# A recommender's attention over a history of 200: a fifth tile of rows fetched by address, a reordered step, and a contraction of the head over 128 rows

## The chip, the cores and the metric

The kernel runs on one core of a Trainium2 chip. The core has a matrix engine (PE, with its weight loads shown as PEld), a vector engine (DVE), an activation engine (ACT), GpSimd (POOL) and a synchronizing engine (SP). ACT, POOL and SP each have a queue of their own on which DMAs are issued in order. The metric is the device time of one execution in microseconds (us). The kernel before has a median of 31618.79 over three runs (31618.49 to 31619.22).

## What is computed

The reference is a "deep interest" ranking model for a batch of B = 16384 with a history of L = 200 items. Embeddings have 64 numbers. For every position l of the history and every sample, an attention unit of 36 hidden values weighs the row of the item; dice normalizes over axis 1 of the hidden values, that is over the batch, for each l by itself.

```python
u = u_emb[user]; it = i_emb[item]; c = c_emb[cate]
h = i_emb[hist]                                   # (200, 16384, 64)
itb = jnp.broadcast_to(it[None], h.shape)
feat = jnp.concatenate([h, itb, h - itb, h * itb], axis=-1)
a = dice(feat @ au_W1 + au_b1, au_alpha, axis=1)  # 36 hidden values
w = a @ au_W2 + au_b2
cur = jnp.sum(w * jax.lax.stop_gradient(h), axis=0)
z = jnp.concatenate([u, it, c, cur], axis=-1)
z = dice(z @ W1 + b1, alpha1, axis=0)
z = dice(z @ W2 + b2, alpha2, axis=0)
return z @ W3 + b3
```

`dice(x)` is `x * (p + alpha * (1 - p))` with p the sigmoid of x normalized by its mean and variance. So 200 x 16384 rows of 256 bytes are to be fetched from a table of 100000 rows, at random places.

## The kernel before

**Tiling.** The batch is cut into 128 tiles of 128 samples. Sixteen tiles (TD) make a chunk c; there are ND = 8 chunks for each l. One chunk of one l is a step, k = 8 l + c, so there are 1600 steps. Steps are software pipelined: in the code of step k, rows of chunk k are fetched, chunk k - 1 is transposed and multiplied, the result of k - 2 is taken out of PSUM and measured, and chunk k - LAG, whose normalization is known by then, gets its gate and its weights (LAG is 10). The first 180 l run in a hardware loop, `tc.For_i`, of 45 l an iteration; the other 20 follow it, and then the head. The order of the instructions on every engine is the order in which the code issues them (`tc.manual_schedule`).

**Rows.** `gather` (line 125) is one indirect DMA on POOL's queue that fetches the 128 rows of one tile into a slice of `rows[k % 5]`. In four of the eight chunks (SIDES) the last tile is not gathered in this way. Its rows are fetched one at a time by address: `scale_addresses` (L146) multiplies the indices by the bytes of a row, `addresses` (L268) loads some of them into registers of an engine, and each row is a DMA of 256 bytes. SP does so for the chunks 1 and 5 (`rows_by_sync`, L280, 16 registers at a load) into the buffers `side`; it is asked one or two chunks ahead by `ask`, 32 rows a step. ACT does so for the chunks 3 and 7 (`rows_by_scalar`, L291, 8 registers at a load) into `aside`, 16 rows behind the gate and 16 behind hidden of each step. ACT's rows count on a semaphore `landed`, which `await_rows_by_scalar` (L297 to L299) waits for and clears. `turn` copies the finished tile into `rows` (L339, ACT) right ahead of the transposes.

**A step.** In the order of issue: `fetch(k)` on POOL; `gate(k - LAG)`, a sigmoid on ACT (L312) from `xs` to PSUM `pg`; `weights(k - LAG)`, y = pg * xs on DVE (L315) and eight passes of PE into `wb`; half of ACT's rows; `hidden(k - 2)` on ACT (L323), px with the bias into `xs[k % XR]`, and `measure` (L328), two statistics on DVE; the other half of ACT's rows; `turn(k - 1)`, the copy, four 64x512 transposes on DVE (L154) into `hT[k % LAG]`, four PE passes with a unit matrix into `ph` and eight into `px` (L159, `layer`); `weigh(k - LAG)` on DVE (L319, L320), which adds weight times row to `curT`; `product(k - 1)`, hm = ph * itT on DVE (L345) and four passes into `px`. At the last chunk of an l `moments` (L351 to L365 on DVE, then a root on ACT at L168 and L169, L170 on DVE) gives scale and shift for the gate.

**Buffers.** Five `rows`, LAG = 10 `hT`, XR = 9 `xs`, one `px`, `ph`, `pg` and `wb` in PSUM.

**Head.** 256 gathers for users and categories, the first layer (`head_layer`), its moments (L503 to L511), and then for each of eight chunks `dice` (L522 on ACT, L523 and L524 on DVE), the second layer (L538 with `w2a` over 128 rows, L539 with `w2b` over a quarter of 32 rows), L541 on ACT and statistics (L467). The third layer follows (L159 again) and the output.

Of the kernel before, what the change touches and what calls it, by code (L numbers as in the profile page):

```python
# [14 lines left out]
P = 128  # L15
D = 64
EPS = 1e-8
CH = 512
# [1 line left out]
CD = 2 * CH  # L20
LPB = 45
ROWS = 5
LAG = 10
XR = 9
IDX = 3
BY_SP = (1, 5)
BY_ACT = (3, 7)
SIDES = (1, 3, 5, 7)
LOAD = 16
GROUP = 8  # L30
ROW = 4 * D
U8 = mybir.dt.uint8

# [2 lines left out]
def din_kernel(  # L36
# [32 lines left out]
    ZA = P // 2  # L69
    ZB = Z1 - ZA  # L70
    NS = len(SIDES)
    NB, NA = len(BY_SP), len(BY_ACT)
    serial = iter(range(10**6))
    NC = NT - NS
    BODY = L - L % LPB if L > LPB else 0
# [6 lines left out]
    def make(name, *shape, dt=F32):  # L82
        return const.tile(list(shape), dt, name=name)
# [29 lines left out]
    idx = [make(f"idx{i}", P, NC, dt=I32) for i in range(IDX)]  # L113
    ids = [make(f"ids{i}", P, NT, dt=I32) for i in range(3)]
    side = [make(f"side{i}", P, D) for i in range(3)]
    aside = [make(f"aside{i}", P, D) for i in range(3)]
    landed = [tc.alloc_semaphore(f"landed{i}") for i in range(3)]
    addrs = make("addrs", 2 * S + 1, NS * P, dt=I32)
    addr = [addrs[i * S : i * S + 1] for i in range(3)]
# [98 lines left out]
    w1a = make("w1a", P, 4, P)  # L218
    w1b = make("w1b", P, 4, S)
    w2a = make("w2a", P, P)  # L220
    w2b = make("w2b", P, P)
    w3 = make("w3", P, 4, P)
    b1a = make("b1a", P, 1)
    b1b = make("b1b", S, 1)
# [9 lines left out]
    def head_weights():  # L234
        for t in (w1a, w1b, w2a, w2b, w3, bias2, al2):
            nc.vector.memset(t, 0.0)
        w1 = W1.rearrange("(f d) z -> d f z", d=D)
        for e in range(2):
            for g in range(2):
                r, d = quarter(e, g), ts(e, S)  # L240
                nc.sync.dma_start(w1a[r, :, ts(g, ZA)], w1[d, :, :ZA])
                nc.sync.dma_start(w1b[r, :, ts(g, ZB)], w1[d, :, ZA:])
        for g in range(2):
            nc.sync.dma_start(w2a[ts(g, ZA), g * ZA : g * ZA + Z2], W2[:ZA])
            nc.sync.dma_start(b1a[ts(g, ZA)], col(b1)[:ZA])
            nc.sync.dma_start(ala[ts(g, ZA)], col(alpha1)[:ZA])
            nc.sync.dma_start(b1b[ts(g, ZB)], col(b1)[ZA:])
            nc.sync.dma_start(bias2[g * ZA : g * ZA + Z2], col(b2))
            nc.sync.dma_start(al2[g * ZA : g * ZA + Z2], col(alpha2))
            for j in range(4):  # L250
                r = slice(j * S + g * ZB, j * S + (g + 1) * ZB)
                nc.sync.dma_start(w2b[r, g * ZA : g * ZA + Z2], W2[ZA:])
                w = j * S + g * ZO
                nc.sync.dma_start(w3[g * ZA : g * ZA + Z2, j, w : w + ZO], W3)
                nc.sync.dma_start(alb[r], col(alpha1)[ZA:])
        nc.sync.dma_start(bias3, b3.partition_broadcast(P))
        for t, u in ((ala, al1a), (alb, al1b), (al2, al12)):
            nc.vector.tensor_scalar(u, t, -1.0, 1.0, ALU.mult, ALU.add)

        for t, n in ((same_a, ZA), (same_b, ZB)):  # L260
            nc.vector.tensor_single_scalar(lane, lanes, n - 1, ALU.bitwise_and)
            nc.vector.tensor_copy(t, lane)
            nc.vector.tensor_scalar(t, t, 0.0, n / P, ALU.is_equal, ALU.mult)

    flat = i_emb.rearrange("v d -> (v d)").bitcast(U8)

    def addresses(l, s, p0, n, engine):
        _, at = nc.values_load_multi_w_load_instructions(  # L268
            addr[l % 3][:, s * P + p0 : s * P + p0 + n],
            engines=(engine,), min_val=0, max_val=ROW * (V - 1),  # L270
            skip_runtime_bounds_check_because="the DMA checks the address against the table",
        )
        return [flat[ds(a, ROW)].rearrange("(o d) -> o d", o=1) for a in at]

    def rows_by_sync(m, part, n):
        l, j = divmod(m, NB)
        s, dst = SIDES.index(BY_SP[j]), side[m % 3].bitcast(U8)
        for p0 in range(part * n, part * n + n, LOAD):
            for j, row in enumerate(addresses(l, s, p0, LOAD, mybir.EngineType.SP)):
                nc.sync.dma_start(dst[p0 + j : p0 + j + 1], row)  # L280


    keys = {}

    def rows_by_scalar(m, part):
        l, j = divmod(m, NA)
        s, dst = SIDES.index(BY_ACT[j]), aside[m % 3].bitcast(U8)
        key = keys.setdefault(m, f"rows{next(serial)}")
        for j, row in enumerate(addresses(l, s, part * GROUP, GROUP, mybir.EngineType.Activation)):
            p = part * GROUP + j  # L290
            dma = nc.scalar.dma_start(dst[p : p + 1], row).then_inc(landed[m % 3], 16)  # L291
            tc.no_tile_sem_insts.add(dma.ins.name)
            tc.add_to_no_dep_group(key, dma.ins)

    def await_rows_by_scalar(m):
        if m in keys:
            fence = nc.scalar.wait_ge(landed[m % 3], 16 * P)  # L297
            tc.declare_fence(fence.ins, group=keys.pop(m))
            nc.scalar.sem_clear(landed[m % 3])  # L299
# [4 lines left out]
    def fetch(k):  # L304
        l, c = divmod(k, ND)
        for n in range(TD - has_side(k)):
            j = column(c, n)
            gather(rows[k % ROWS], idx[l % IDX][:, j : j + 1], n, i_emb)
# [13 lines left out]
    def hidden(k):  # L322
        nc.scalar.activation(xs[k % XR], px, AF.Identity, bias=au_bias)  # L323
# [3 lines left out]
        for i in range(2):  # L327
            nc.vector.bn_stats(stats[l % 3][:, 2 * c + i, :], xs[k % XR][:, ts(i, CH)])  # L328

    def turn(k):  # L330
        if has_side(k):
            l, c = divmod(k, ND)
            if c in BY_ACT:
                m = l * NA + BY_ACT.index(c)
                await_rows_by_scalar(m)
                of = aside[m % 3]
            else:
                of = side[(l * NB + BY_SP.index(c)) % 3]
            nc.scalar.copy(rows[k % ROWS][:, TD - 1], of)  # L339
        transpose(hT[k % LAG], rows[k % ROWS])  # L340
        layer(ph, [(unit, hT[k % LAG])])
        layer(px, [(blk_h, hT[k % LAG]), (blk_i, itT[k % ND])], last=False)
# [25 lines left out]
    def step(k, last=None):  # L368

        def has(j):  # L370
            return last is None or j <= last

        if has(k):
            fetch(k)
        if has(k - LAG):
            gate(k - LAG)
            weights(k - LAG)
        if has(k):
            scalar_rows(k, 0)
        if has(k - 2):  # L380
            hidden(k - 2)
            measure(k - 2)
        if has(k):
            scalar_rows(k, 1)
        if has(k - 1):
            turn(k - 1)
        if has(k - LAG):
            weigh(k - LAG)
        if has(k - 1):
            product(k - 1)  # L390
        if has(k - 2) and (k - 2) % ND == ND - 1:
            moments((k - 2) // ND)

    AHEAD = ND // NB - 1 - BY_SP[0]

    def ask(k, end):
        m, part = divmod(k + 1 + AHEAD, ND // NB)
        if m < end * NB:  # L400
            rows_by_sync(m, part, P * NB // ND)

    def scalar_rows(k, slot):
        m, part = divmod(k, ND // NA)
        n = P * NA // ND // GROUP
        for i in range(n)[slot::2]:
            rows_by_scalar(m, part * n + i)

    def steps(l0, n, end):
        for k in range(n * ND):  # L410
            l, c = divmod(k, ND)
            if c == 0 and l + 1 < end:
                load_hist_ids((l + 1) % IDX, l0 + l + 1)
            if c == 2 and l + 1 < end:
                load_addresses((l + 1) % 3, l0 + l + 1)
            if c == 4 and l + 1 < end:
                scale_addresses((l + 1) % 3)
            ask(k, end)
            step(k)

    with tc.manual_schedule():
# [4 lines left out]
        load_ids(ids[2], r_user)  # L426
        nc.gpsimd.iota(lanes, pattern=[[1, P]], base=P, channel_multiplier=-1)
        attention_weights()
        for t in (*hT, *xs, *side, *aside, hm):
            nc.vector.memset(t, 0.0)  # L430
        for t in curT:
            nc.vector.memset(t, 0.0)
# [14 lines left out]
            if c:  # L447
                transpose(itT[c - 1], rows[(c - 1) % ROWS])
        nc.vector.memset(rows[-1 % ROWS], 0.0)
        for k in range(-1 - AHEAD, 0):  # L450
            ask(k, L)
        head_weights()

    if BODY:
        with tc.For_i(0, BODY, LPB) as l0:  # L455
            with tc.manual_schedule():
                steps(l0, LPB, LPB + 1)
                await_rows_by_scalar(LPB * NA - 1)

    K = (L - BODY) * ND  # L460
    za = [hT[(K - LAG + c) % LAG] for c in range(ND)]
# [28 lines left out]
    with tc.manual_schedule():  # L490
# [36 lines left out]
        z2 = itT  # L527
        na, nb = head_moments(0, same_a), head_moments(1, same_b)
        ab = ucT[:2]
        for j in range(2):  # L530
            dice(ab[j], zb[j], nb, al1b, alb)
        for c in range(ND + 1):
            if c < ND:
                dice(curT[c], za[c], na, al1a, ala)
                q = ts(c % 4, S)
                for h in range(2):
                    cols = ts(h, CH)
                    nc.tensor.matmul(pz[c % 4][:, cols], w2a, curT[c][:, cols], start=True, stop=False)  # L538
                    nc.tensor.matmul(pz[c % 4][:, cols], w2b[q], ab[c // 4][q, cols], start=False, stop=True)  # L539
            if c:  # L540
                nc.scalar.activation(z2[c - 1], pz[(c - 1) % 4], AF.Identity, bias=bias2)  # L541
                measure_head(2, c - 1, z2[c - 1])

        n2 = head_moments(2, same_a)
        for c in range(ND):
# [56 lines left out]
```

## Time and profile before

| what | us |
|---|---|
| median of three runs | 31618.79 |
| the profiled execution | 31616.96 |
| its span | 31615.1 |
| POOL busy | 23766.1 |
| PE busy | 20448.2 |
| DVE busy | 15015.4 |
| ACT busy | 4479.6 |
| DMA engines, mean busy share: POOL's queue, the two others with rows | 11.8%, 0.4% and 0.3% |

Busy time does not count register loads or the issuing of DMAs: the time that ACT and SP spend on issuing rows is in none of these. An ordinary line of a group reads: line, engine, operation, output <- inputs, count | busy us in all, mean ns of one | idle time of the engine before them, and what ended it. "issue" is idle time that ended without a wait for anything that the profile shows. A line of a timeline reads: start and duration in us, engine (with a q: its queue, issuing), line, operation, tiles, how many were merged into the line, and in brackets the idle time before it and who released it. In a line on one place of the code, three times separated by strokes are the minimum, median and maximum in ns.

### The profile page before, as it was taken

How to read it: one execution, taken by the hardware profiler on the slowest of the kernel's cores; microseconds unless marked ns; L12 is line 12 of the kernel's file. 1: busy time of each engine (PE TensorE's matmuls, PEld its weight loads, DVE VectorE, ACT ScalarE, POOL GpSimd, SP SyncE). 2: the span in 40 equal slices, each digit the busy share in tenths (PEclk: the TensorE clock that was granted, in tenths of full speed). 3: DMA queues.
4: the chain of work that ended last, by engine and by line, in shares of the span. 5: the costliest groups of instructions: out<-in, count | busy, mean ns of one | idle time of the engine just before them, and what ended most of it. 6: DMA issues, size and time to landing. Idle time of an engine off the chain costs nothing. (4 is left out here: it accounts for less than half of the span.)

```text
span 31615.1 us, 357535 instructions
## 1 busy us (share of the span) xinstructions
PE 20448.2 (65%) x38864; PEld 8357.2 (26%) x38864; DVE 15015.4 (47%) x18963; ACT 4479.6 (14%) x4670; POOL 23766.1 (75%) x25189
## 2 busy tenths in 40 slices
PE   5666666666666666666666666666666666666666
PEld 2222222222222222222222222222222222222222
DVE  4444444444444444444444444444444444444443
ACT  1111111111111111111111111111111111111111
POOL 7777777777777777777777777777777777777776
PEclk7888888888888888888888888888888888888887
DMA  1111111111111111111111111111111111111111
GB/s 29 28 28 28 28 28 28 28 28 28 28 28 28 28 28 28 28 28 28 28 28 28 28 28 28 28 28 28 28 28 28 28 28 28 28 28 28 28 28 23
DMA packets 1050292, 890.26 MB, mean 28 GB/s; under 512 B 644640, under 2 KB 644640, under 8 KB 1047784
## 3 DMA queue, kind: packets, MB, share of 16 engines
q0 software_dynamic: 805888, 826.84, 11.8%
q1 hardware_dynamic: 138920, 27.05, 0.4%
q10 hardware_dynamic: 102976, 13.32, 0.3%
q14 instruction: 2202, 18.04, 0.2%
q8 instruction: 306, 5.01, 0.1%
HBM read 865.03 MB, written 0.13 MB: 27 GB/s over the span
## 5 line engine op out<-in xcount | busy, mean ns | idle before, releaser
L125 POOL DMA_INDIRECT rows<-in_L_rec_i_emb,idx x24800 | 23403.2, 944 | 7593.5 <-issue 7032.1
L159 PE MATMUL ph<-hT,unit 128*128 128x512 f32 x6404 | 5658.4, 1029 | 10498.9 <-DVE hT L154 10498.9
L154 DVE STREAM_TRANSPOSE hT<-rows 64x512 f32<-64x512 f32 x6404 | 4518.8, 706 | 8256.8 <-DMA rows<-in_L_rec_i_emb,idx 4150.3
L328 DVE BATCH_NORM_STATS2 st<-xs 128x6 f32<-128x512 f32 x3204 | 2060.4, 685 | 7172.9 <-ACT xs L323 7172.9
L159 PEld LDWEIGHTS ph<-hT,unit 128*128 128x128 f32 x6404 | 1688.5, 295 | 13506.4 <-DVE hT L154 13334.4
L159 PE MATMUL px<-hT,blk_h 128*128 128x512 f32 x6404 | 3936.6, 702 | 0.0
L323 ACT ACTIVATE xs<-px,au_bias 128x1024 f32<-128x1024 f32 x1602 | 1784.3, 1114 | 14626.1 <-PE px L159 12323.9
L159 PE MATMUL wb<-y,blk_p 128*128 128x512 f32 x6440 | 3329.8, 599 | 455.3 <-DVE y L315 455.3
L159 PE MATMUL px<-itT,blk_i 128*128 128x512 f32 x6404 | 3368.8, 608 | 0.0
L159 PE MATMUL wb<-xs,blk_x 128*128 128x512 f32 x6440 | 3307.3, 595 | 51.5 <-PEq L455 39.9
L159 PE MATMUL px<-hm,blk_m 128*128 128x512 f32 x6408 | 3013.0, 592 | 40.5 <-DVE hm L430 40.5
L312 ACT ACTIVATE pg<-xs,sh,rs 128x1024 f32<-128x1024 f32 x1610 | 1939.8, 1205 | 3751.2 <-issue 2579.9
L315 DVE TENSOR_TENSOR y<-pg,xs 128x1024 f32<-128x1024 f32 x1610 | 1956.6, 1215 | 512.9 <-ACT pg L312 508.6
L159 PEld LDWEIGHTS px<-hT,blk_h 128*128 128x128 f32 x6404 | 1566.7, 245 | 2295.1 <-issue 2294.6
L319 DVE SCALAR_TENSOR_TENSOR wb<-wb,au_bias,hT 128x1024 f32<-128x1024 f32 x1610 | 2080.5, 1292 | 88.2 <-PE wb L159 36.0
L320 DVE TENSOR_TENSOR curT<-wb,curT 128x1024 f32<-128x1024 f32 x1610 | 1970.8, 1224 | 54.8
L345 DVE TENSOR_TENSOR hm<-ph,itT 128x1024 f32<-128x1024 f32 x1601 | 1941.2, 1212 | 0.0
L159 PEld LDWEIGHTS px<-itT,blk_i 128*128 128x128 f32 x6404 | 1374.9, 215 | 1925.3 <-issue 1925.3
L159 PEld LDWEIGHTS wb<-y,blk_p 128*128 128x128 f32 x6440 | 1212.0, 191 | 2081.7 <-issue 1445.9
L159 PEld LDWEIGHTS wb<-xs,blk_x 128*128 128x128 f32 x6440 | 1228.3, 191 | 1603.9 <-issue 1597.9
L159 PEld LDWEIGHTS px<-hm,blk_m 128*128 128x128 f32 x6408 | 1218.1, 190 | 1573.0 <-issue 1424.7
L339 ACT COPY rows<-aside 128x64 f32<-128x64 f32 x401 | 97.9, 244 | 2659.6 <-DMA aside<-in_L_rec_i_emb 2525.7
(155 smaller groups left out, 2171.5 us busy)
## 6 DMA issues: line engine op xcount, KB each, us to landing
aside<-in_L_rec_i_emb ACTq DMA_DIRECT2D x51200, 0.2 KB
side<-in_L_rec_i_emb SPq DMA_DIRECT2D x51200, 0.2 KB
rows<-in_L_rec_i_emb,idx POOLq DMA_INDIRECT x24800, 2.4
idx<-in_r_hist SPq DMA_DIRECT2D x200, 62.0 KB
addrs<-in_r_hist SPq DMA_DIRECT2D x200, 2.0 KB
rows<-in_L_rec_i_emb,ids POOLq DMA_INDIRECT x128, 2.4
rows<-in_L_rec_c_emb,ids POOLq DMA_INDIRECT x128, 2.4
rows<-in_L_rec_u_emb,ids POOLq DMA_INDIRECT x128, 2.4
```

What stands on the lines that cost most here:

```text
L125: nc.gpsimd.indirect_dma_start(out=dst[:, n, :], out_offset=None, in_=table, in_offset=bass.IndirectOffsetOnAxis(ap=ids, axis=0),)
L154: nc.vector.transpose(by_tile(dst[ts(e, D)], i), of[ts(i, D), :, ts(e, S)])
L159: nc.tensor.matmul(dst[:, ts(i, CH)], lhsT, rhs[:, ts(i, CH)], start=(first and j == 0), stop=(last and j == len(pairs) - 1), skip_group_c ...
L312: nc.scalar.activation(pg, xs[k % XR], AF.Sigmoid, bias=shifts[i], scale=rstds[i])
L315: nc.vector.tensor_mul(y, pg, xs[k % XR])
L319: nc.vector.scalar_tensor_tensor(wb, wb, au_bias2, hT[k % LAG], ALU.add, ALU.mult)
L320: nc.vector.tensor_add(curT[k % ND], wb, curT[k % ND])
L323: nc.scalar.activation(xs[k % XR], px, AF.Identity, bias=au_bias)
L328: nc.vector.bn_stats(stats[l % 3][:, 2 * c + i, :], xs[k % XR][:, ts(i, CH)])
L339: nc.scalar.copy(rows[k % ROWS][:, TD - 1], of)
L345: nc.vector.tensor_mul(hm, ph, itT[k % ND])
```

## The change

Chunks with a side tile become 1, 3, 4, 6 and 7: five tiles of each l are fetched by address, and 123 are gathered. SP and ACT both fetch rows of every such tile: each step has 80 rows, of which SP issues the first 40 and ACT the last 40, in loads of 20 registers. All count on `landed`, the buffers are three `side`, and `aside` is gone. The rows of a tile are no longer asked for ahead: those of step k are issued in step k, at the end of what ACT has in it. The copy has a function of its own, `place`, ahead of the rows.

In a step `hidden` now comes first; in the step where an l ends, its statistics and moments follow at once. Then come the gate, the copy, the rows, the transposes with their passes, the statistics of other steps, the product, and at the end `weights` and `weigh`. LAG is 9 and XR is 8.

In the head `w2b` has four planes of 128 rows, of which one quarter is not zero, so that the second matmul contracts over 128 rows as the first does; the `dice` of `ab` is made where it is needed, behind the first pass of a group of four chunks, and the result is taken out of PSUM two chunks later instead of one.

```diff
-LAG = 10
-XR = 9
+LAG = 9
+XR = 8
-BY_SP = (1, 5)
-BY_ACT = (3, 7)
-SIDES = (1, 3, 5, 7)
-LOAD = 16
-GROUP = 8
+SIDES = (1, 3, 4, 6, 7)
+LOAD = 20
...
-    w2b = make("w2b", P, P)
+    w2b = make("w2b", P, 4, P)
...
+    PER_STEP = NS * P // ND
+
+    def rows_by_address(k):
+        l, s = divmod(k, ND)
+        for i, (engine, issue) in enumerate(
+            ((mybir.EngineType.SP, nc.sync), (mybir.EngineType.Activation, nc.scalar))
+        ):
+            n = PER_STEP // 2
+            for r0 in range(s * PER_STEP + i * n, s * PER_STEP + (i + 1) * n, LOAD):
+                _, at = nc.values_load_multi_w_load_instructions(
+                    addr[l % 3][:, r0 : r0 + LOAD],
+                    engines=(engine,), min_val=0, max_val=ROW * (V - 1),
...
+                for r, a in enumerate(at, r0):
+                    m, p = l * NS + r // P, r % P
+                    key = keys.setdefault(m, f"rows{next(serial)}")
+                    dma = issue.dma_start(
+                        side[m % 3].bitcast(U8)[p : p + 1],
+                        flat[ds(a, ROW)].rearrange("(o d) -> o d", o=1),
+                    ).then_inc(landed[m % 3], 16)
...
-    def turn(k):
+    def place(k):
         if has_side(k):
             l, c = divmod(k, ND)
...
-            nc.scalar.copy(rows[k % ROWS][:, TD - 1], of)
+            m = l * NS + SIDES.index(c)
+            await_rows(m)
+            nc.scalar.copy(rows[k % ROWS][:, TD - 1], side[m % 3])
+
+    def turn(k):
         transpose(hT[k % LAG], rows[k % ROWS])
...
+        ends = (k - 2) % ND == ND - 1
         if has(k):
             fetch(k)
+        if has(k - 2):
+            hidden(k - 2)
+            if ends:
+                measure(k - 2)
+                moments((k - 2) // ND)
         if has(k - LAG):
             gate(k - LAG)
-            weights(k - LAG)
+        if has(k - 1):
+            place(k - 1)
         if has(k):
-            scalar_rows(k, 0)
-        if has(k - 2):
-            hidden(k - 2)
-            measure(k - 2)
-        if has(k):
-            scalar_rows(k, 1)
+            rows_by_address(k)
         if has(k - 1):
             turn(k - 1)
-        if has(k - LAG):
-            weigh(k - LAG)
+        if has(k - 2) and not ends:
+            measure(k - 2)
         if has(k - 1):
             product(k - 1)
-        if has(k - 2) and (k - 2) % ND == ND - 1:
-            moments((k - 2) // ND)
...
+        if has(k - LAG):
+            weights(k - LAG)
+            weigh(k - LAG)
...
-            ask(k, end)
             step(k)
...
-        for j in range(2):
-            dice(ab[j], zb[j], nb, al1b, alb)
-        for c in range(ND + 1):
+        for c in range(ND + 2):
             if c < ND:
                 dice(curT[c], za[c], na, al1a, ala)
...
+                layer(pz[c % 4], [(w2a, curT[c])], last=False)
+                if c % 4 == 0:
+                    dice(ab[c // 4], zb[c // 4], nb, al1b, alb)
+                layer(pz[c % 4], [(w2b[:, c % 4], ab[c // 4])], first=False)
+            if c >= 2:
+                nc.scalar.activation(z2[c - 2], pz[(c - 2) % 4], AF.Identity, bias=bias2)
+                measure_head(2, c - 2, z2[c - 2])
```

More of the change, by code (lines that the diff above doesn't have):

```diff
@@ L71, in din_kernel @@
     NS = len(SIDES)
-    NB, NA = len(BY_SP), len(BY_ACT)
     serial = iter(range(10**6))
@@ L115, in din_kernel @@
     side = [make(f"side{i}", P, D) for i in range(3)]
-    aside = [make(f"aside{i}", P, D) for i in range(3)]
     landed = [tc.alloc_semaphore(f"landed{i}") for i in range(3)]
@@ L251, in head_weights @@
                 r = slice(j * S + g * ZB, j * S + (g + 1) * ZB)
-                nc.sync.dma_start(w2b[r, g * ZA : g * ZA + Z2], W2[ZA:])
+                nc.sync.dma_start(w2b[r, j, g * ZA : g * ZA + Z2], W2[ZA:])
                 w = j * S + g * ZO
@@ L265, in din_kernel @@
     flat = i_emb.rearrange("v d -> (v d)").bitcast(U8)
[L267 to L280, printed above, removed]
@@ L283, in din_kernel @@
-    keys = {}
[L285 to L293, printed above, removed]
@@ L295, in await_rows_by_scalar @@
-    def await_rows_by_scalar(m):
+    keys = {}
+    PER_STEP = NS * P // ND
[9 more added lines that the diff above has]
+                    engines=(engine,), min_val=0, max_val=ROW * (V - 1),
+                    skip_runtime_bounds_check_because="the DMA checks the address against the table",
+                )
+                for r, a in enumerate(at, r0):
[5 more added lines that the diff above has]
+                    ).then_inc(landed[m % 3], 16)
+                    tc.no_tile_sem_insts.add(dma.ins.name)
+                    tc.add_to_no_dep_group(key, dma.ins)
@@ L296, in await_rows_by_scalar, with await_rows @@
+    def await_rows(m):
         if m in keys:
@@ L328, in measure @@
             nc.vector.bn_stats(stats[l % 3][:, 2 * c + i, :], xs[k % XR][:, ts(i, CH)])
-    def turn(k):
+    def place(k):
         if has_side(k):
             l, c = divmod(k, ND)
[L333 to L339, printed above, removed]
+            m = l * NS + SIDES.index(c)
+            await_rows(m)
+            nc.scalar.copy(rows[k % ROWS][:, TD - 1], side[m % 3])
+    def turn(k):
         transpose(hT[k % LAG], rows[k % ROWS])
@@ L371, in has @@
             return last is None or j <= last
+        ends = (k - 2) % ND == ND - 1
         if has(k):
             fetch(k)
+        if has(k - 2):
[3 more added lines that the diff above has]
+                moments((k - 2) // ND)
         if has(k - LAG):
             gate(k - LAG)
-            weights(k - LAG)
+        if has(k - 1):
+            place(k - 1)
         if has(k):
-            scalar_rows(k, 0)
-        if has(k - 2):
-            hidden(k - 2)
-            measure(k - 2)
-        if has(k):
-            scalar_rows(k, 1)
+            rows_by_address(k)
         if has(k - 1):
             turn(k - 1)
-        if has(k - LAG):
-            weigh(k - LAG)
+        if has(k - 2) and not ends:
+            measure(k - 2)
         if has(k - 1):
             product(k - 1)
-        if has(k - 2) and (k - 2) % ND == ND - 1:
-            moments((k - 2) // ND)
[L396 to L407, printed above, removed]
+        if has(k - LAG):
+            weights(k - LAG)
+            weigh(k - LAG)
     def steps(l0, n, end):
@@ L428, in din_kernel @@
         attention_weights()
-        for t in (*hT, *xs, *side, *aside, hm):
+        for t in (*hT, *xs, *side, hm):
             nc.vector.memset(t, 0.0)
@@ L449, in din_kernel @@
         nc.vector.memset(rows[-1 % ROWS], 0.0)
-        for k in range(-1 - AHEAD, 0):
-            ask(k, L)
         head_weights()
@@ L457, in din_kernel @@
                 steps(l0, LPB, LPB + 1)
-                await_rows_by_scalar(LPB * NA - 1)
+                await_rows(LPB * NS - 1)
     K = (L - BODY) * ND
@@ L529, in din_kernel @@
         ab = ucT[:2]
-        for j in range(2):
-            dice(ab[j], zb[j], nb, al1b, alb)
-        for c in range(ND + 1):
+        for c in range(ND + 2):
             if c < ND:
                 dice(curT[c], za[c], na, al1a, ala)
[L535 to L542, printed above, removed]
+                layer(pz[c % 4], [(w2a, curT[c])], last=False)
[5 more added lines that the diff above has]
+                measure_head(2, c - 2, z2[c - 2])
         n2 = head_moments(2, same_a)
```

## The prediction

> **What bounds the kernel now.** I read the busy times first, then the costliest groups, then the timeline of one ordinary step, then that of a loop end and of the last 120 us.
>
> The page's busy times, slices and costliest group:
>
> ```profile
> PE 20448.2 (65%) x38864; PEld 8357.2 (26%) x38864; DVE 15015.4 (47%) x18963; ACT 4479.6 (14%) x4670; POOL 23766.1 (75%) x25189
> ...
> POOL 7777777777777777777777777777777777777776
> PEclk7888888888888888888888888888888888888887
> ...
> L125 POOL DMA_INDIRECT rows<-in_L_rec_i_emb,idx x24800 | 23403.2, 944 | 7593.5 <-issue 7032.1
> ```
>
> 75% does not look like a bound, but the idle time is put down to "issue": the next gather follows the last without a wait. (23403.2 + 7593.5) / 24800 = 1.250 us for each gather; 24800 of them are 30997 us of the 31615. POOL is a metronome, and nothing else in the loop is. It stops only at the ends of the hardware loop:
>
> ```profile
> 7129.46 0.94 POOL L125 DMA_INDIRECT rows<-in_L_rec_i_emb,idx  x1 [0.30 <-issue]
> 7139.70 0.94 POOL L125 DMA_INDIRECT rows<-in_L_rec_i_emb,idx  x1 [9.30 <-issue]
> ```
>
> In between, each l lasts 124 gathers, 155.0 us, and a step 18.75 or 20 us. The rows fetched by address have to fit beside that. What one of them costs a queue is in the timeline, in pieces where a queue runs without a pause:
>
> ```profile
> 14997.77 25.14 SPq L280 DMA_DIRECT2D side<-in_L_rec_i_emb  x64
> ...
> 15025.69 1.21 ACT L312 ACTIVATE pg<-xs,sh,rs 128x1024 f32<-128x1024 f32 x1 [6.47 <-issue]
> 15026.62 6.26 ACTq L291 DMA_DIRECT2D aside<-in_L_rec_i_emb  x16
> ...
> 15038.74 2.64 ACTq L291 DMA_DIRECT2D aside<-in_L_rec_i_emb  x8
> ```
>
> The line of the address loads, by queue (minimum/median/maximum ns), gives the load of 8 registers on ACT and of 16 on SP:
>
> ```profile
> L268 ACTq TENSOR_LOAD <-addrs x6400: 709/817/1073, 51.3 to 31136.3; - x194
> L268 SPq TENSOR_LOAD <-addrs x3200: 1132/1230/1459, 51.3 to 31016.3; - x189
> ```
>
> Eight rows take 2.64 us, 0.33 each; sixteen with one load between them take 6.26, so a load with its gaps is 6.26 - 2 x 2.64 = 0.98 (0.82 and 0.16). The ACTIVATE at 15025.69 lasts until 15026.90, yet rows go out from 15026.62: the activations run beside the queue, and only its waits and issues fill the queue.
>
> The third clock is the chain of DVE and PE within a step:
>
> ```profile
> 15007.62 2.88 DVE L154 STREAM_TRANSPOSE hT<-rows 64x512 f32<-64x512 f32 x4 [5.32 <-ACT rows L339]
> 15009.10 3.76 PE L159 MATMUL ph<-hT,unit 128*128 128x512 f32 x4 [5.89 <-DVE hT L154]
> ...
> 15020.42 1.02 PE L159 MATMUL wb<-y,blk_p 128*128 128x512 f32 x2
> ```
>
> From the first transpose to the end of the last wb pass it is 15021.4 - 15007.6 = 13.8 us.
>
> The last 120 us, where POOL has nothing left to do:
>
> ```profile
> 31504.35 2.05 PE L538 MATMUL px<-curT,w2a 128*128 128x512 f32 x2 [9.48 <-issue]
> ...
> 31566.43 2.07 PE L539 MATMUL wb<-ucT,w2b 32*128 32x512 f32 x2
> ...
> 31580.38 9.12 PE L159 MATMUL px<-curT,w 128*128 128x512 f32 x16 [6.80 <-DVE curT L524]
> ```
>
> The second layer's 64 passes run from 31504.35 to 31568.5, 1.00 us a pass, back to back; the third layer's 16 passes, all of 128 rows, take 0.57 on average.
>
> **The change part by part.**
>
> *One gather less for each l.* 200 x 1.250 = 250.0 us off POOL's row, if POOL stays the metronome. Nothing hides this: POOL was without waits, so each gather removed is time removed. After, an l has 123 gathers, 153.7 us, 19.2 a step.
>
> *Rows on the two queues.* 40 rows a step each instead of 32, in two loads of 20. The load is in no row: bounded below by the 16-register load (1.23), above by two and a half times the 8-register one (2.04); from 0.82 and 1.23 a register is 0.05, so I take 1.44. Then 2 x (1.44 + 0.16) + 40 x 0.33 = 16.4 us a step, on both queues (SP: 64 rows in 25.14 with at least three loads of about 1.4 among them, also 0.33 a row). ACT's other issues and waits that find their semaphore ready are about 0.5: 16.9 of 19.2. Nothing of this lies on the path while that holds. SP has no other work but one load of indices and one of addresses an l; before it was 32 x 0.33 + 2 x 1.39 = 13.3. If the price of a row is what fills up, 0.33 may be wrong from 0.31 (the 0.22 of one issue with its move and gaps) to 0.42 (6.68 / 16, the dearest stretch in that timeline, load included): 15.6 to 20.0. I take 0.33, since it comes from clean pieces of both queues.
>
> *ACT's order.* Its queue now has hidden, gate, the copy of the side rows, then all rows of the step. Behind the copy's wait for landings stand the 40 rows, and behind these the next hidden, which frees px for PE and whose xs DVE measures. Rows of tile c = 7 end with ACT's last row of the step; one step later their landing is awaited, about 2 us (the gathers' landings in the chain are 2.4) once an l. With XR 8 hidden(k-2) writes the buffer that weights(k-10) has read, and those wb passes now stand at the end of a step. So the loop is transposes, 13.8 us to the last wb pass, hidden 1.1, gate 1.2, copy 0.24: 16.4, with semaphores 16.7 us. DVE's own loop (13.8, then L319 1.29 and L320 1.22) is 16.3. All three are below 19.2.
>
> *The moments first.* Once an l hidden, two L328 (1.3), L351 to L365 (2.2 and gaps), the root with its table load and L169/L170 come before gate: about 7 us in which ACT issues no row. ACT: 8 x 16.9 + 7 + 2 = 144 us an l; the chain: 8 x 16.7 + 7 = 141; POOL: 153.7. Ten us are left in an l, 6%. They cover the whole reordering at nothing; without them each us over is 200 us of the time. Five rows buffers let POOL run four steps ahead, so a late step is absorbed.
>
> *Fewer buffers (LAG, XR, aside), w2b four times as wide, three more index loads, SP's rows no longer asked for ahead of the loop.* Memsets in the prelude change by 2 us under 160 us of gathers of items; nothing. At a loop end POOL waits 9.3 us for its own last landings and its drain; ACT's last rows are out before, since hidden runs ahead of the gathers. Between 3 us less and 3 more at four ends: 12 either way, taken as 0.
>
> *The second layer of the head.* w2b with 32 rows alternating with w2a's 128 becomes 128 rows throughout, still 64 passes. In the step px with blk_h and blk_i, also alternating, pairs start 0.86 apart: 0.43 a pass. The first five passes of a stretch take 0.85 (granted clock half, by the third layer's rows). dice of ab moves behind the first curT: PE starts at 31496.9 + 1.24 + 0.81 + 1.23 = 31500.3, 4 us sooner. 5 x 0.85 + 59 x 0.43 = 29.6: end at 31530 instead of 31568.5, 38 less. DVE has 10 x 2.04 + 7 x 1.29 = 29.4 us there, so it is about level and the next limit; I take 37. Bounds: all passes at the half clock 54.7 us, gain 14; passes still at 1.00, gain 4.
>
> Two rules speak against these parts. The Trainium skill's "TensorEngine Tiling (Array Packing)", section When to Use Tiling, would have a contraction of 32 rows tiled by rows for up to four times the speed; by it the old form should win, and the sum would be 31367 or more. The rows say 1.00 against 0.43 a pass, since neighbours here differ in form. Its "DMA: Bandwidth & Descriptors", section Specifications, asks for at least 512 B a transfer; by it 25600 more rows of 256 B waste engine time, which at this page's 0.7% of the engines for both queues would still cost nothing, and the sum stays.
>
> *Sum.* Against the profiled execution (31616.96, of which the span is 31615.1): 31617.0 - 250.0 - 37 = 31330. The median of the three runs stands 1.8 above it: 31332, 0.91% less.
>
> **The rivals.**
>
> *ACT's queue becomes the bound (slower).* It decides when 8 x (3.7 + 40p) + 9 passes 153.7, at p = 0.36 a row, and is slower than before by 0.2% from p = 0.37. At 0.40 an l is 166.6: (166.6 - 155.0) x 200 - 37 = +2280, 33900. For it: a bound only 6% away, two queues issuing at once for longer, 6.68 for sixteen rows once. Against: SP held 0.33 over 64 rows while ACT was issuing.
>
> *The chain of copy, transposes, wb passes and hidden becomes the bound (slower).* It is longer than before, since weights now come behind product and XR is one less. It decides at 18.3 us a step; I have 16.7. At 20 an l is 167: (167 - 155) x 200 - 37 = +2360, 33980. For it: the wait for xs is new. Against: DVE 47% and PE 65%.
>
> *POOL stays the bound but loses some of it.* Late landings or loop ends that wait for ACT's rows, say 20 us at each of four ends or half a us an l: 31400 to 31480.
>
> *The cadence is not POOL's own.* If the gathers were paced by what the DMA engines take, removing one would stretch the others and only the head's 37 remained: 31582. Against: the gathers of the head, with no rows beside them, come in the same 1.25.
>
> **How the numbers follow.** Forecast 0.79 (its own range 31305 to 31370: the head's bounds, four loop ends); partial loss 0.06; ACT's queue 0.08; the chain 0.05; cadence 0.02. 8 in 10 is the forecast with the partial loss: 31300 to 31470. What a measurement can tell from no change is 0.2%, 63 us. Faster: 0.79 + 0.06 + half of 0.02 = 0.86; slower: ACT and chain, less what lands near zero, 0.12; same 0.02.
>
> **What would show it.** POOL's row with x24600 and a mean of 944, idle still to "issue"; POOL's gaps 0.30 with no new releaser; rows on both queues 0.33 apart; ACT's copy waiting for landings at most 2 us once an l; in the tail 64 passes in some 30 us with PE no longer stepping by 1.00. Wrong if POOL's idle names DVE transposes (a full set of rows buffers), or ACT's hidden starts with no wait for PE in every step.

## The result and the profile after

The changed kernel takes 31326.86 us (median of four runs, 31323.99 to 31328.28), the kernel before 31618.9: a ratio of 0.9908, 95% interval 0.989 to 0.9925, 292 us less. The forecast was 31332. Four of the runs below were made together on another chip, on which the kernel before itself takes 48919 us; their times are read against that number only.

The profiled executions take 31616.96 and 31327.14, 289.8 less. Where it went, from the two traces:

| stretch | before | after | difference |
|---|---|---|---|
| first to last gather of the history | 30996.4 | 30744.8 | -251.6 |
| of it, four loop ends beyond the cadence | 26.1 | 18.3 | -7.8 |
| last gather of the head to the end | 136.4 | 98.1 | -38.3 |

The page of after, with the busy times and the lines that answer those of before:

```profile
PE 20675.6 (66%) x38856; PEld 8537.2 (27%) x38856; DVE 15152.4 (48%) x18955; ACT 4382.9 (14%) x4874; POOL 23580.4 (75%) x24989
...
L120 POOL DMA_INDIRECT rows<-in_L_rec_i_emb,idx x24600 | 23217.6, 944 | 7527.6 <-issue 7237.9
```

POOL is still the metronome: (23217.6 + 7527.6) / 24600 = 1.250 us, idle still put down to "issue". The timeline of POOL at the first loop end of after:

```profile
7074.98 0.94 POOL L120 DMA_INDIRECT rows<-in_L_rec_i_emb,idx  x1 [0.30 <-issue]
7082.08 0.94 POOL L120 DMA_INDIRECT rows<-in_L_rec_i_emb,idx  x1 [6.15 <-issue]
```

It stands still for 6.15 us where it was 9.30. The load of 20 registers (by queue, minimum/median/maximum ns), and one step on ACT, from the timeline:

```profile
L274 SPq TENSOR_LOAD <-addrs x3200: 1355/1454/1706, 50.5 to 30840.8; - x189
L274 ACTq TENSOR_LOAD <-addrs x3200: 1409/1452/1798, 168.2 to 30893.6; - x189
```

```profile
15013.66 1.11 ACT L317 ACTIVATE xs<-px,au_bias 128x1024 f32<-128x1024 f32 x1 [15.34 <-PE wb L154]
15014.67 1.20 ACT L306 ACTIVATE pg<-xs,sh,rs 128x1024 f32<-128x1024 f32 x1
15015.44 0.53 ACTq L282 DMA_DIRECT2D side<-in_L_rec_i_emb  x1
15015.80 0.23 ACT L329 COPY rows<-side 128x64 f32<-128x64 f32 x1
15016.05 14.30 ACTq L282 DMA_DIRECT2D side<-in_L_rec_i_emb  x39
15033.36 1.11 ACT L317 ACTIVATE xs<-px,au_bias 128x1024 f32<-128x1024 f32 x1 [17.33 <-PE wb L154]
```

The rows are out at 15030.35 and the next hidden starts at 15033.36: 3.0 us in which ACT's queue waits for PE's wb passes. The bracket's 17.33 us is idle time of the activation unit, most of it under the issuing of rows; it isn't the slack.

The second layer of the head on PE, from the timeline (first and last lines):

```profile
31250.00 3.69 PE L154 MATMUL px<-curT,w2a 128*128 128x512 f32 x4 [5.06 <-issue]
31253.53 1.88 PE L154 MATMUL px<-ucT,w2b 128*128 128x512 f32 x4
...
31275.85 1.88 PE L154 MATMUL wb<-curT,w2a 128*128 128x512 f32 x4
31277.56 1.88 PE L154 MATMUL wb<-ucT,w2b 128*128 128x512 f32 x4
```

From 31250.00 to 31279.44, 29.4 us for the 64 passes; four of them start 1.72 apart, 0.43 each. What the price of a pass is made of shows in the granted clock, the share of PE's full clock that the chip allowed. Two stretches of the second layer, one of before and one of after (from:to, length, then busy time and instructions of PE, PEld, DVE, ACT and POOL, granted clock, DMA share, GB/s):

```profile
31504.00:31569.00 65.00, 64.15 (x64) 16.01 (x64) 22.84 (x29) 15.03 (x14) 0.00 (x0) 0.50 0.00 0
31254.00:31279.00 25.00, 25.00 (x60) 10.98 (x58) 22.11 (x28) 14.56 (x13) 0.00 (x0) 1.00 0.00 1
```

In the old layer PE is busy for 64.15 of 65 us, and yet its granted clock is 0.50 all the time. In the new one it is 1.00 from 3.5 us on. Before that, the first four passes, over 128 rows at the half clock, take 0.88 us each where the old ones took 1.00. So I estimate that some 8 of the 35 us (64 x 0.12) are the form of the passes at the same clock, and the other 27 are the clock. Why the clock stayed at half beside passes over 32 rows was not tried.

### The profile page after: what moved, and what is told of

The parts are those of the page before. It is cut to its first block, busy times and chain, and to the rows that moved or that the text cites. A ratio compares the mean times of both kernels' runs of the same rounds, so it can differ in the third digit from the quotient of the medians.

```text
span 31325.4 us, 404768 instructions
## 1 busy us (share of the span) xinstructions
PE 20675.6 (66%) x38856; PEld 8537.2 (27%) x38856; DVE 15152.4 (48%) x18955; ACT 4382.9 (14%) x4874; POOL 23580.4 (75%) x24989
## 5 line engine op out<-in xcount | busy, mean ns | idle before, releaser
L120 POOL DMA_INDIRECT rows<-in_L_rec_i_emb,idx x24600 | 23217.6, 944 | 7527.6 <-issue 7237.9
L154 PE MATMUL ph<-hT,unit 128*128 128x512 f32 x6404 | 5985.6, 1090 | 10436.2 <-DVE hT L149 10423.5
L154 PEld LDWEIGHTS ph<-hT,unit 128*128 128x128 f32 x6404 | 1799.7, 311 | 13493.8 <-DVE hT L149 13296.9
L154 PEld LDWEIGHTS px<-hT,blk_h 128*128 128x128 f32 x6404 | 1631.8, 255 | 2412.2 <-issue 2412.2
```

What stands on the lines that cost most here:

```text
L120: nc.gpsimd.indirect_dma_start(out=dst[:, n, :], out_offset=None, in_=table, in_offset=bass.IndirectOffsetOnAxis(ap=ids, axis=0),)
L154: nc.tensor.matmul(dst[:, ts(i, CH)], lhsT, rhs[:, ts(i, CH)], start=(first and j == 0), stop=(last and j == len(pairs) - 1), skip_group_c ...
```

## The experiments

The theory: POOL's gathers set the time, so each gather removed is 1.25 us; the queues of SP and ACT, and the chain through DVE and PE, lie just under that; the head's 38 us stand by themselves. The main rivals: the order of the step is what gained, or the two queues have more or less room than worked out.

**The head alone.**

```diff
 kernel before, and:
...
+                layer(pz[c % 4], [(w2a, curT[c])], last=False)
+                if c % 4 == 0:
+                    dice(ab[c // 4], zb[c // 4], nb, al1b, alb)
+                layer(pz[c % 4], [(w2b[:, c % 4], ab[c // 4])], first=False)
...
```

> The kernel before with only the head's part: w2b over 128 rows, dice of ab behind the first pass, results taken out two chunks later. By my theory the parts add, and this one is the shorter tail: 31618.9 - 38 = 31581, the 64 passes in 29 to 30 us, POOL's row as before (24800 gathers). By the rival that the tail became shorter through the reordered steps (LAG 9, a drain that ends sooner), the time stays at 31619.

Measured: 31587.69 beside 31627.61 for the kernel before on the same chip, ratio 0.9988 (0.9978 to 0.9997), 39.9 us less. From the last gather to the end it is 98.8 us instead of 136.4; the 64 passes take 30.6, with a granted clock of 1.00 from 5.8 us on. The parts add, and this one owes nothing to the step.

**The new order with four tiles.**

```diff
 changed kernel, and:
-SIDES = (1, 3, 4, 6, 7)
-LOAD = 20
+SIDES = (1, 3, 5, 7)
+LOAD = 16
```

> The changed kernel with four tiles by address for each l (1, 3, 5, 7; 32 rows a step on each queue, loads of 16): the reordered step and the head's part without the fifth tile. By my theory the order is worth nothing by itself: 24800 gathers again, before less the head's 38 and less what the loop ends got shorter by (8 us): 31573. By the rival that the new order removes stalls of its own, it is well below that, up to all of the 250 us: 31327.

Measured: 31588.45 beside 31627.61, ratio 0.9988 (0.9978 to 0.9997), 39.2 us less, the same as the head alone. The group of POOL's gathers in this run:

```profile
L120 POOL DMA_INDIRECT rows<-in_L_rec_i_emb,idx x24800 | 23403.2, 944 | 7593.7 <-issue 7216.7
```

So order, sharing of each tile by both queues, LAG and XR are together worth nothing with four tiles; none of them was tried alone. The gathers of the history take 30996.6 us here and 30744.8 in the changed kernel: the fifth tile is the whole of the 251.6. The loop ends here stand 26.1 us beyond the cadence, as before; the 8 us go with the fifth tile, and why was not tried.

**The old order with five tiles.**

```diff
 changed kernel, and:
-LAG = 9
-XR = 8
+LAG = 10
+XR = 9
...
+        if has(k - LAG):
+            gate(k - LAG)
+            weights(k - LAG)
+        if has(k):
+            rows_by_address(k, 0)
+        if has(k - 2):
+            hidden(k - 2)
+            measure(k - 2)
+        if has(k):
+            rows_by_address(k, 1)
+        if has(k - 1):
+            place(k - 1)
+            turn(k - 1)
+        if has(k - LAG):
+            weigh(k - LAG)
...
```

Of `rows_by_address(k, 0)` come SP's 40 rows and ACT's first 20, of `rows_by_address(k, 1)` ACT's other 20.

> Five tiles by address as in the changed kernel, but the step in the order of before: gate and weights first, ACT's rows in two halves of 20 behind the gate and behind hidden, the copy behind all rows and right ahead of the transposes, moments at the end; LAG 10, XR 9. By my theory the reordering is what makes room for the fifth tile: in a step with a side tile copy, transposes and product (10.8 us until px is there) come in series with hidden's wait and the second half of the rows (8.2), 19.3 us; in the other three steps the queue has 16.9; moments at the end hold ACT for some 12 us: 5 x 19.3 + 3 x 16.9 + 14 = 161 us an l against 153.7, so 32790. By the rival that the order is worth nothing here either, as with four tiles, 31335.

Measured: 31327.29 beside 31619.27, ratio 0.9908 (0.9891 to 0.9924): the changed kernel's time. My theory that the reordering makes room for the fifth tile fell. Its timeline on ACT, with the first and second copy of a side tile and then a step without one:

```profile
15006.19 0.24 ACT L330 COPY rows<-side 128x64 f32<-128x64 f32 x1 [6.94 <-DMA side<-in_L_rec_i_emb]
...
15018.24 1.11 ACT L318 ACTIVATE xs<-px,au_bias 128x1024 f32<-128x1024 f32 x1 [10.70 <-PE px L154]
...
15026.37 0.24 ACT L330 COPY rows<-side 128x64 f32<-128x64 f32 x1 [7.01 <-DMA side<-in_L_rec_i_emb]
...
15036.87 1.11 ACT L318 ACTIVATE xs<-px,au_bias 128x1024 f32<-128x1024 f32 x1 [9.15 <-PE px L154]
...
15045.24 1.21 ACT L307 ACTIVATE pg<-xs,sh,rs 128x1024 f32<-128x1024 f32 x1 [7.26 <-issue]
```

The series is there: from copy to copy 20.2 us (in the median 20.0 and 19.2 for the two such pairs of an l), against my 19.3. Two other terms of the sum were too large. The moments hold ACT's queue for 6 us (in this stretch of the trace from a table load at 15101.7 to the root at 15107.7), not for the 12 that I took. And a chunk without a side tile doesn't wait for rows: its transposes begin 13.1, 14.4 and 15.9 us (medians) after those of the chunk before it, where I took 16.9 for such a step, and they stand only 1.8 to 2.2 us behind its last gather. So the step catches up with POOL three times in an l. It fits with less to spare: for the five chunks with a side tile the first transpose comes 5 to 9 us (medians, by chunk) after the last gather, where the changed kernel has 1.7 to 3.2 for all.

**ACT's rows in loads of 8, and SP's.**

```diff
 changed kernel, and on one of the two engines:
-LOAD = 20
+LOADS = (20, 8)   # SP, ACT; and (8, 20)
```

> The changed kernel with ACT's 40 rows of a step in five loads of 8 registers instead of two of 20; SP keeps 20. In the trace of before a load of 8 with its rows takes 3.6 us, so ACT's queue has 18.1 us of rows and 0.5 of other issues in a step: 18.6 x 8 + 9 = 158 us an l against POOL's 153.7. By my theory (a queue that is 6% below the bound) the queue now ends last: about 4 us an l, 32150, POOL's idle time naming the transposes. By the rival that the queue has more room than I worked out, because only its rows and not the waits add up, it stays at 31327.

> The same on SP alone: SP's 40 rows in five loads of 8, ACT keeps 20. SP then has some 18.1 us of rows in a step and nothing else, 146 us an l with its index loads, under 153.7. By my theory nothing changes: 31327, with SP's waits for ACT shorter. By the rival that what counts is the rate of both queues together (rows landing, the DMA engines), it costs the same as the loads of 8 on ACT: 32150.

Measured, beside 31627.61: on ACT 31589.45 (31581.18 to 31642.95), ratio 0.9989 (0.998 to 0.9999); on SP 31333.88, ratio 0.9907 (0.9891 to 0.9924). On the same chip the same loads cost 256 us more on one queue than on the other. The timeline of ACT in the profiled run with loads of 8 on ACT, the longest of its ten (31642.95):

```profile
20005.44 16.45 ACTq L282 DMA_DIRECT2D side<-in_L_rec_i_emb  x37
20022.01 1.11 ACT L317 ACTIVATE xs<-px,au_bias 128x1024 f32<-128x1024 f32 x1 [16.41 <-DVE wb L313]
...
20024.28 16.02 ACTq L282 DMA_DIRECT2D side<-in_L_rec_i_emb  x37
20040.43 1.11 ACT L317 ACTIVATE xs<-px,au_bias 128x1024 f32<-128x1024 f32 x1 [16.04 <-issue]
```

Hidden starts 0.12 us after the last row: the queue is full. The transposes fall behind the gathers, by up to 78 us, which is four steps and as much as the buffers allow. Where POOL pays for it is in its own timeline, here at the first two loop ends:

```profile
7124.23 0.94 POOL L120 DMA_INDIRECT rows<-in_L_rec_i_emb,idx  x1 [0.31 <-issue]
7197.52 0.94 POOL L120 DMA_INDIRECT rows<-in_L_rec_i_emb,idx  x1 [72.34 <-issue]
...
14111.77 0.95 POOL L120 DMA_INDIRECT rows<-in_L_rec_i_emb,idx  x1 [0.30 <-issue]
14180.80 0.94 POOL L120 DMA_INDIRECT rows<-in_L_rec_i_emb,idx  x1 [68.08 <-issue]
```

Within a loop of 45 l the `rows` buffers hide most of the delay: POOL goes on at its cadence, and only in the first loop did it wait for buffers, some 47 us in all. At each of the four loop ends it stands still for about 70 us (69.0 to 73.3 from gather to gather) until ACT's queue has caught up. These ends cost 262 us more than those of the changed kernel, about the 256 by which the median is longer. An l took 155.3 us in the mean, where POOL alone needs 153.7; I had 158, and so 32150. The queue did become the bound, with my sum 2% too high. The theory that ACT's queue is the next bound is shown, and that SP's is not.

**ACT's rows in loads of 10, and all addresses shifted by 8 bytes.**

```diff
 changed kernel, and:
-LOAD = 20
+LOADS = (20, 10)   # SP, ACT
```

> ACT's rows in four loads of 10, between the five loads of 8 (31589, ACT's queue the bound) and the two of 20. Four groups take 4 x 4.4 = 17.6 us a step, 0.5 less than five groups of 8, so 4 us an l less than the 155.3 that the loads of 8 took: 151.3, under POOL's 153.7. By the theory of a threshold, POOL is the metronome again and the time is back at 31335, with nothing left of the 255 us. By the rival that what the loads cost is paid in proportion all the way, half of it stays: 31460.

Measured: 36403.42 beside 31619.27, ratio 1.1512 (1.1493 to 1.1531). Neither theory: fewer, larger loads cost some 4800 us more than the loads of 8 did. The register loads in this run:

```profile
L274 ACTq TENSOR_LOAD <-addrs x6400: 1154/1897/2733, 168.3 to 36073.5; - x194
L274 SPq TENSOR_LOAD <-addrs x3200: 1356/1454/1707, 50.6 to 36006.9; - x189
```

In the median a load of 10 takes longer than one of 20. One by one they alternate: those that start at a multiple of 16 bytes of the addresses' row take 1.16 or 1.27 us, those 8 bytes past it 2.46. Hence the next run, in which nothing but the start changes:

```diff
 changed kernel, and:
-    addrs = make("addrs", 2 * S + 1, NS * P, dt=I32)
-    addr = [addrs[i * S : i * S + 1] for i in range(3)]
+    addrs = make("addrs", 2 * S + 1, 2 + NS * P, dt=I32)
+    addr = [addrs[i * S : i * S + 1, 2:] for i in range(3)]
```

> The changed kernel with the addresses two columns (8 bytes) further in their tile, so that every load of 20 registers begins 8 bytes past a multiple of 16. In the run with loads of 10 on ACT, loads at a multiple of 16 bytes took 1.16 to 1.27 us and those 8 bytes past it 2.46. By the theory that the start address is what cost 5000 us there: each load of 20 takes 1.25 to 2.5 us more, ACT's step 19.4 to 21.9, 160 to 180 us an l: 32600 to 36500. By the rival that loads of 10 registers are slow as such, whatever their address: 31327, loads still 1.45.

Measured, on the chip where the kernel before takes 48919.26: 54268.37, ratio 1.1087 (1.1067 to 1.1107). Its loads, and then those of the run with nine xs on the same chip, whose addresses start as in the changed kernel:

```profile
L274 SPq TENSOR_LOAD <-addrs x3200: 742/4322/4589, 110.3 to 53844.5; - x189
L274 ACTq TENSOR_LOAD <-addrs x3200: 960/4457/4740, 179.4 to 53831.8; - x189
```

```profile
L274 SPq TENSOR_LOAD <-addrs x3200: 3/1451/1727, 110.3 to 48800.9; - x189
L274 ACTq TENSOR_LOAD <-addrs x3200: 3/1433/1824, 180.0 to 48789.4; - x189
```

The median load goes from 1.45 to 4.4 us, three times, by 8 bytes, beyond the 2.5 us more that I had allowed. The address theory is shown by the loads; its effect in time is seen only as 54268 against 49286 on this chip, in the run with nine xs.

**Six tiles in every l.**

```diff
 changed kernel, and:
-SIDES = (1, 3, 4, 6, 7)
-LOAD = 20
+SIDES = (1, 2, 3, 5, 6, 7)
+LOAD = 24
```

> Six tiles by address for each l, 48 rows a step on each queue in two loads of 24; 122 gathers. By my theory ACT's queue is then the bound: two groups of 24 take 19.3 us, with 0.5 of others 19.8 x 8 + 9 = 167 us an l, or 164.5 if the sum is too high by as much as it was for the loads of 8: 33500 to 34000, slower than before the change. By the rival that POOL's gathers are all that counts: another 250 us less, 31085.

Measured: 34683.85 beside 31619.27, ratio 1.0968 (1.095 to 1.0987), 700 us beyond the upper end. POOL's gathers and what it waits for, in groups:

```profile
L120 POOL DMA_INDIRECT rows<-in_L_rec_i_emb,idx x24400 | 23034.5, 944 | 11052.8 <-issue 7126.2 <-DVE hT L149 3591.3 <-DMA rows<-in_L_rec_i_emb,idx 166.8
```

POOL is no longer without waits: the transposes, late behind ACT's queue, hold its buffers. An l lasts 170.4 us. Two groups of 24 took 2 x 9.75 = 19.5 us where I had 19.3, and ACT's queue waited a little more than the sum allowed: 170 in place of 167. The bound turned, as the rival of ACT's queue had it, though here by more rows and not by dearer ones.

**A sixth tile in every third l.** If the bound is a mean over the buffers, the room left can be spent in part.

```diff
 changed kernel, and:
+SIDES = (1, 3, 4, 5, 6, 7)
+EXTRA = 5
...
+    def sides(l):
+        return tuple(c for c in SIDES if c != EXTRA or l % 3 == 1)
...
+        PER_STEP = len(sides(l)) * P // ND
+        LOAD = PER_STEP // 4
```

> A sixth tile (of chunk 5) by address in every third l alone (67 of 200), 48 rows a step there, and five tiles in the others. By my theory the bound is the mean over what the five rows buffers can hold back: ACT's queue has 2 x 144.2 + 167.4 = 456 us in three l, POOL 368 gathers of 1.25, 460. So 67 gathers less: 31335 - 84 = 31251. By the rival that a late l is not caught up, each of the 67 costs what the six tiles cost in an l, 11 to 13 us: 31335 + 67 x 11, about 32100.

Measured: 31251.55 (31251.06 to 31251.79) beside 31619.27, ratio 0.9884 (0.9867 to 0.99). That is 75.7 us less than five tiles on the same chip (31327.29, the old-order run), and faster than both kernels. Of the 84 us of 67 gathers, 4 are lost at the loop ends (22.2 us beyond the cadence in place of 18.0), most of the rest in gaps a little longer than 1.25. ACT's queue spends 14 us an l without issuing, where the changed kernel has 23; six of these are the moments.

**On the other chip.** Three more questions went there.

```diff
 nine xs: changed kernel, and:
-XR = 8
+XR = 9
 loops of 90: the sixth tile in every third l, and:
-LPB = 45
+LPB = 90
 old order: the sixth tile in every third l, and the order, LAG and XR as in the old order above
```

> The changed kernel with nine xs buffers instead of eight, so that hidden of one step no longer writes what the wb passes of the step before have read. In the changed kernel ACT's hidden names PE's wb in 1387 of 1600 steps. By my theory that wait is slack of a queue that has time left, under POOL: the releaser changes to PE's px and the time stays at 31327. By the rival that this chain is near the bound and costs some of the gathers: up to 30 us less.

> The sixth tile in a third of the l (31251.6) with hardware loops of 90 l instead of 45, so two ends of four. Each end stops POOL for 4 to 6 us beyond its cadence: by my theory two of them less are 31251 - 11 = 31240. By the rival that a longer body has to be fetched anew and costs it elsewhere: 31251 or more.

> The sixth tile in a third of the l, with the step in the order of before (LAG 10, XR 9; ACT's rows in halves of 24 or 20). With five tiles the order made no difference, and ACT's queue waited 22 us an l in either. If the order is worth nothing at the margin as well: 31251. If the reordering buys room that five tiles didn't need, because in the old order copy, transposes, px and hidden stand in series with half of the rows, then here, where the queue has some 4 us an l left, it shows: an l with six tiles then lasts 8 x 21 + 14 = 182 us, 27 more than five-tile l with 10 us of room each can take back in part: 67 x 10 = 670 us more, 31900.

Measured, beside 48919.26: 49286.36 with nine xs (ratio 1.0074, 1.0057 to 1.0091), 50736.57 with loops of 90 (1.0372, 1.0348 to 1.0396), 53357.22 with the old order (1.0905, 1.0887 to 1.0923). The page of the run with nine xs says what this chip does:

```profile
PE 20804.5 (42%) x38856; PEld 8526.4 (17%) x38856; DVE 15079.2 (31%) x18956; ACT 4409.0 (9%) x4874; POOL 23570.4 (48%) x24989
...
L120 POOL DMA_INDIRECT rows<-in_L_rec_i_emb,idx x24600 | 23207.6, 943 | 25299.3 <-DVE hT L149 17669.3
```

Every engine works as long as elsewhere; gathers still take 943 ns. But the queues of SP and ACT run in part at 0.7 us an instruction, for some 15 us at a time, so that rows come 0.77 us apart in the mean, loads and waits included, where the changed kernel elsewhere has 0.49 (the median is 0.32 in both). In the four runs traced there POOL waits for the transposes for 17669 us and more, behind these queues; of the kernel before there is no trace from this chip. What slows the queues is open. The questions of nine xs and of loop ends can't be read there. The old order cost 2620 us more than the new one (the loops differ too, two ends of some 6 us); this is the only place where the order made a difference, and it is shown on this chip alone.

## Why the prediction was right

- *One gather less for each l, 250.0.* Measured 251.6 on POOL's row, of which 7.8 are the loop ends and the cadence gave back 6 (0.2 ns a gather over 24600); that these two nearly cancel is luck. The fifth tile alone, with the order held (five against four tiles), is the whole of it.
- *16.4 us of rows a step.* A group of 20 takes 8.2 us in after, load 1.45 where I took 1.44: 16.4. The queue's slack in an ordinary step was 2.3 by my sum and 3.0 in the step shown.
- *Ten us left in an l.* ACT's queue issues nothing for 23 us of 153.7, about 9 of these in the step with the moments: 14 left. The loads of 8 add 15 us an l (in a step five groups of 3.66 us for two of 8.2) and overran it. My 9 us for moments and landing were too many: in the run with loads of 8 ACT's queue stops for 5.7 us around the moments, and in the changed kernel the copy waited for landings 16.3 us in the whole program, 11 times, where I had allowed 2 us in every l.
- *The chain, 16.7 us.* From the first transpose to the end of the last wb pass it is 14.2 us in the median, where I had 13.8. The wait that I named came, hidden on PE's wb in 1387 of 1600 steps, and cost nothing, since it lies in that slack: in the run with the old order hidden names wb 118 times, and the time is the same.
- *The head, 37.* 38.3 in the trace and 39.9 alone. The start at 31250.00 is 3.45 us after the first sigmoid at 31246.55; I had 3.28 (which gives 31500.2 and not 31500.3 in the sum). The 64 passes took 29.4 us against 29.6. The reason was half right: I put 1.00 against 0.43 down to neighbours that differ in form, but the row with 1.00 ran at a granted clock of 0.50 and the one with 0.43 at 1.00. I took the rise of the clock after five passes from the third layer, with 54.7 us as the bound without it; that the clock of the old layer was at half I didn't see, and here the number came out with some luck.
- *Loop ends, 0 within 12.* They gave 8.
- *The two rules.* The Trainium skill's "TensorEngine Tiling (Array Packing)", When to Use Tiling, would tile a contraction over a quarter of the rows. Here, with one quarter at a time between passes over 128 rows, a pass took 1.00 us against 0.43, at the clocks just named, and the run with the head alone shows 39.9 us for this and the moved `dice` together. No run has several quarters at work at once. What "DMA: Bandwidth & Descriptors", Specifications, asks (512 B a transfer) cost nothing that the time shows: the queues with the 256-byte rows have 0.5% and 0.3% of the engines after the change.

What was off were theories made after the result: that the order carried the gain, by a term of 14 us for moments and landing, where the moments take 6, and that loads of 10 lie between 8 and 20.

## What to carry to other kernels

When one engine runs without a wait, count its instructions: each one taken away is worth its full cadence until the next queue fills, and that point can be worked out from the price of one issue and one register load. Work moved to another queue is free up to there and dear beyond it, 256 us here for two us more in a step, most of which were free, and a part of the l can take the room that all of them can't (a sixth tile in every third l). Buffers hide a queue that is a little too slow until all engines have to meet, here at the end of a hardware loop; look there for the loss. Issuing time is in no busy share; read it from the queue's own lines. And read the price of a matmul pass together with its granted clock: half of it may be the clock.

## What was not expected of the hardware

- PE was busy for 64.15 of 65 us with passes over 128 and over 32 rows in turn, at a granted clock of 0.50; with passes over 128 rows alone the clock was 1.00 within 6 us.
- A register load of 20 from an address 8 bytes past a multiple of 16 takes 4.4 us in place of 1.45; one of 10 takes 2.46 in place of 1.2. Loads of 10 on ACT made the kernel 15% slower than the one before the change.
- On one chip the queues of SP and ACT ran for stretches at 0.7 us an instruction, with all engines' own work unchanged (seen with nine xs); the kernel before took 48919 us there instead of 31619.
- POOL's stop at a loop end was 2 us shorter with five tiles than with four, for a reason not found.
